# Output product of layer 0 from seven products of half blocks, in 19 of its 32 steps

## The chip, the cores and the metric

The kernel runs on one core of a Trainium2 chip. A core has TensorE (matmuls, PE in the profile), VectorE (DVE), ScalarE (ACT), GpSimd (POOL) and SyncE (SP, which issues DMAs). The metric is the device time of one execution in microseconds (us). Before the change the median of three runs is 2060.91 us (2059.85 to 2061.62).

## What is computed

Two transformer-like layers over 4 sequences of 512 tokens with 512 features, all in f32. Layer 0 adds to its input an attention and a mixture of experts. The attention has 16 heads of 128: every head sees a local window (the token's own block of 128 and the one before) and the eight best of 128 compressed entries; the two contexts are averaged. All heads together go through the output matrix Wo:

```python
merged = (ctx_sparse + ctx_local) * 0.5
out = merged.transpose(0, 2, 1, 3).reshape(Bq, Sq, NH * D) @ Wo + bo
...
x = x + _L0_attn_ref(xn, ...) + _L0_ffn_ref(xn, L0_ffn_Wr, L0_ffn_We, L0_ffn_be)
```

The product with Wo (2048 rows, 512 columns) is what the change touches. Layer 1, another attention and a second mixture of experts, stays as it is.

## The kernel before, in words

**Steps.** Layer 0's attention runs as 32 steps (list `steps`). A step i is a pair (g, b): g is one of 8 pairs of heads, b one of 4 sequences, and b runs fastest, so four steps share the weights of a head pair. In step i the kernel makes the scores and contexts of step i, the projections (queries, keys, values) of step i + 1, and pieces of the mixture of experts. From step 5 to step 22 each step handles two slots of 128 sorted token rows: `turn` (L517 to L519) transposes the gathered rows, `apply` (L529, L532) multiplies them with the expert's weights. GpSimd gathers rows and weights with indirect DMAs (L481) ahead of use. From step 23 on the experts' results are added up instead (L545, L852).

**A step in order.** `scores` (L749) makes for a head the compressed scores sp (L758) and the local scores st in two halves (L767). From sp, VectorE makes s (L761), finds the eight best (MAX, L779, and MATCH_REPLACE, L780) and masks the rest (L782 and L783, two operations on SBUF), and ScalarE takes the exponential (L784). From st, ScalarE makes lT (L771), and GpSimd multiplies it with a mask (L775). `context` (L798) multiplies with the values (L809 to L814), normalizes on ScalarE and VectorE (L818 to L827). `turn_context` (L831) transposes the context of a head on TensorE (trc, L834), and ScalarE copies it to cT[:, h, :] (L835). cT has 128 partitions (the head's features), 2 heads, 512 tokens.

**The output product.** `output` (L837) runs four times a step, once for each block of 128 tokens: two matmuls of 128 x 512, one for each head, accumulate in a PSUM bank op (L842), and VectorE adds op to acc (L845). acc is the residual stream, kept in SBUF for all 16 blocks of 128 tokens. Wo's part of the head pair is loaded once in four steps by `load_out` (L107, L109) into a single buffer; SyncE's queue holds that DMA until the step before has read the old one.

**Projections.** They are made from seven products of half blocks already (`project`, L650), each with two matmuls of 384 columns (L675). `first` makes the first four PSUM results of a step; VectorE's L710 and L711 take them out. `second`, `third`, `fourth` and `fifth` follow; the last takes its results out at L739 and rotates the keys (L585 to L588) after ScalarE has summed their squares (L575); GpSimd turns the sums into roots (L577, L578). In steps 5 to 23 the transposes of queries and keys (trq L695, trk L701) stand ahead of `fifth`. The sums of weight blocks that the seven products need are made by VectorE in `combine_weights` (L119), in steps with b = 2.

**PSUM.** `psum(tag, name)` hands out banks of 512 f32 for each partition: three buffers for "mm" (projections, expert products, output products), three for "sc" (scores, contexts), two for "tr" (transposes). A matmul into a fourth "mm" tile waits until VectorE has read one of the three.

**What sets the order.** The program text gives a priority; a scheduler at build time puts each engine's instructions in order, and each engine then runs its own queue strictly in that order, waiting on semaphores. The order is thus known before a run. TensorE's matmuls in f32 appear as two records each in the profile, each with a weight load (PEld).

Of the kernel before, what the change touches and what calls it, by code (L numbers as in the profile page):

```python
# [12 lines left out]
F32 = mybir.dt.float32  # L13
I32 = mybir.dt.int32
AF = mybir.ActivationFunctionType
ALU = mybir.AluOpType
# [4 lines left out]
P = 128  # L21
B, S, HID = 4, 512, 512
T = B * S
NT = T // P
TC = S // P
# [24 lines left out]
def two_layers(ctx: ExitStack, tc: tile.TileContext, a: dict, out: bass.AP, large: bass.AP):  # L50
# [3 lines left out]
    nc = tc.nc  # L54
    V, G, A, PE = nc.vector, nc.gpsimd, nc.scalar, nc.tensor
# [8 lines left out]
    wpool = layer0.enter_context(tc.tile_pool(name="wattn", bufs=2))  # L64
    const0 = layer0.enter_context(tc.tile_pool(name="const0", bufs=1))
    qp = layer0.enter_context(tc.tile_pool(name="qkv", bufs=2))
# [6 lines left out]
    def psum(tag, name):  # L73
        return ps.tile([P, 512], F32, tag=tag, name=name, bufs={"mm": 3, "sc": 3, "tr": 2}[tag])

    def load(pool, name, shape, src):
        t = pool.tile(shape, F32, tag=name, name=name, bufs=1)
        nc.sync.dma_start(out=t, in_=src)
        return t
# [8 lines left out]
    def load_block(g, nm, between=None):  # L88


        w = wpool.tile([P, KC, 3 * D], F32, tag=nm, name=f"{nm}_{g}", bufs=1 if nm == "wA" else 2)
        for f in range(2):
            nc.sync.dma_start(out=w[:, ts(f, 2), :],
                              in_=a[nm][g, ts(f, 2 * P), :].rearrange("(k p) c -> p k c", p=P))
            if between:
                between(nm, f)
        return w

    def load_later(g):

        w = load_block(g, "wB")
        b2 = wpool.tile([P, 2, 3 * D], F32, tag="b2", name=f"b2_{g}")
        for i, nm in enumerate(("bA", "bB")):
            nc.sync.dma_start(out=b2[:, i, :], in_=a[nm][g].partition_broadcast(P))
        return [[None, w], b2]

    def load_out(g):  # L107
        wo = wpool.tile([P, HG, HID], F32, tag="Wo", name=f"Wo_{g}", bufs=1)
        nc.sync.dma_start(out=wo, in_=a["Wo"][ds(g * HG * D, HG * D), :].rearrange("(h p) c -> p h c", p=P))  # L109
        return wo  # L110
# [11 lines left out]
            tc.keep_in_program_order(d)  # L122
        sums_w[g] = t2_, t3_, t4_

    sums_w, out_w = {}, {}
    wk = wv = bkv = cmask = lmask = eidx = row = part = None


    acc = keep.tile([P, NT, HID], F32, tag="acc", name="acc")
# [8 lines left out]
    def load_x(n):  # L138
        nc.sync.dma_start(out=acc[:, n, :], in_=x_v[:, n, :])
# [61 lines left out]
    def tables():  # L201

        for hs, w in ((0, 0), (1, 0), (2, 1)):
            tc.keep_in_program_order(G.tensor_tensor(t1[:, :, hs, :], cos[:, 0:TC], own_(w, TC, 0, R), ALU.mult))
            for half, other in ((0, 1), (1, 0)):
                tc.keep_in_program_order(G.tensor_tensor(t2[:, :, hs, ts(half, 32)], sin[:, 0:TC, ts(half, 32)], own_(w, TC, 32 * other, 32), ALU.mult))
# [252 lines left out]
    class Experts:  # L459
# [53 lines left out]
        def turn(self, i):  # L513
            x = self.x[i]
            tr = self.bank("tr", f"trm_{self.r.name}_{i}")
            for k in range(KC):
                PE.transpose(tr[:, ts(k, P)], x[:, ts(k, P)], ident)  # L517
            xT = self.pool.tile([P, KC, P], F32, tag="xT", name=f"xT_{self.r.name}_{i}")
            A.copy(xT, tr.rearrange("p (k t) -> p k t", k=KC))  # L519
            self.x[i] = xT  # L520
# [117 lines left out]
    steps = [(g, b) for g in range(NH // HG) for b in range(B)]  # L638
# [4 lines left out]
    def load_sums(i):  # L643

        for n in range(4):
            xs[n] = wk0.tile([P, 2, 256], F32, tag=f"x{n}", name=f"x{n}_{i}", bufs=1)
            if i >= B:
                nc.sync.dma_start(out=xs[n].rearrange("p k t -> p (k t)"), in_=xsd[steps[i][1], n])
# [182 lines left out]
    def turn_context(i, h, ctx_, cT):  # L831
        tr = psum("tr", f"trc_{i}_{h}")
        for t in range(TC):
            PE.transpose(tr[:, ts(t, P)], ctx_[:, t, :], ident)  # L834
        A.copy(cT[:, h, :], tr)  # L835

    def output(i, t, cT):  # L837
        g, b = steps[i]
        wo = out_w[g]
        op = psum("mm", f"op_{g}_{b}_{t}")  # L840
        for h in range(HG):
            PE.matmul(op, lhsT=cT[:, h, ts(t, P)], rhs=wo[:, h, :],  # L842
                      start=(h == 0), stop=(h == HG - 1))
        n = b * TC + t
        V.tensor_tensor(acc[:, n, :], acc[:, n, :], op, ALU.add)  # L845

    def combine(ex, n):
        rs = ex.gather(n)

        def add():  # L850
            for k in range(2):
                tc.keep_in_program_order(V.scalar_tensor_tensor(  # L852
                    acc[:, n, :], rs[k], ex.r.gate[:, k, n : n + 1], acc[:, n, :], ALU.mult, ALU.add
                ))
        return add
# [29 lines left out]
    def start_sequence(n):  # L885
        for f in layernorm(n, sp0, psum, n >= TC):
            f()
# [4 lines left out]
    for b in range(1, B):  # L892
        i = b - 2
# [77 lines left out]
    for n in range(3 * TC):  # L971
        i, t = 29 + n // TC, n % TC
        last = t + 2 if t < 3 else 5
        if i + 1 == len(steps) and t == 3:
            last = 4
# [14 lines left out]
    def rest():  # L990
        nonlocal wk, wv, bkv, cmask, lmask, eidx, row, part
        start_sequence(2)
        start_sequence(3)
        tables()
        for n in range(TC, TC + 2):
            load_x(n)
        wk = load(sp0, "wk", [P, KC, D], a["Wk"].rearrange("(k p) d -> p k d", p=P))
        wv = load(sp0, "wv", [P, KC, D], a["Wv"].rearrange("(k p) d -> p k d", p=P))
        bkv = sp0.tile([P, 2, D], F32, tag="bkv", name="bkv", bufs=1)
        nc.sync.dma_start(out=bkv[:, 0, :], in_=a["bk"].partition_broadcast(P))  # L1000
        nc.sync.dma_start(out=bkv[:, 1, :], in_=a["bv"].partition_broadcast(P))
        for n in range(TC + 2, 2 * TC):
            load_x(n)
        out_w[0] = load_out(0)
        cmask = load(const0, "cmask", [P, SEEN[TC - 1].stop], a["c_cmask_seen"])
        lmask = load(const0, "lmask", [P, 2, 2, P], a["c_lmask01"])
        for n in range(2 * TC, NT):
            load_x(n)
        eidx = load(const, "eidx", [P, E], a["c_eidx"])
        row = load(const, "row", [P, P], a["c_row"])  # L1010
        part = load(const, "part", [P, 1], a["c_part"])
# [25 lines left out]
    for i, (g, b) in enumerate(steps):  # L1037
        if b == 0:
            if g:
                out_w[g] = load_out(g)  # L1040
            if g + 1 < NH // HG:
                groups[g + 1] = load_later(g + 1)
        more = i + 1 < len(steps)
        turn_last = turn_keys
        now = qkT
        cT = qp.tile([P, HG, S], F32, tag="cT", name=f"cT_{g}_{b}", bufs=1)
        nc.sync.dma_start(out=cv0s[i % 2][96:P, 0:D], in_=cv[0:32, b, 0:D])
        em0, lT0 = scores(i, 0, now)
        turn_last(1)
        if more:  # L1050
            load_sums(i + 1)
            qkT, sums_x, first, second, third, fourth, fifth, turn_queries, turn_keys = project(i + 1)
            first()
            sums_x()
            if b == 2 and g + 1 in groups:
                groups[g + 1][0][0] = load_block(g + 1, "wA")
        run0((i, 0))
        em1, lT1 = scores(i, 1, now)
        sT0 = turn(i, 0, em0)
        run0((i, 1))  # L1060
        if more:
            second(0)
            turn_queries(0)
        ctx0 = context(i, 0, lT0, sT0, lv)
        if more:
            second(1)
        sT1 = turn(i, 1, em1)
        if more:
            third()
        if b == 2 and g + 1 in groups:  # L1070
            combine_weights(g + 1)
        run0((i, 2))
        ctx1 = context(i, 1, lT1, sT1, lv)
        turn_context(i, 0, ctx0, cT)
        run0((i, 3))
        if more:
            fourth()


            if 5 <= i < 24:  # L1080
                turn_queries(1)
                turn_keys(0)
                fifth()
            else:
                fifth()
        turn_context(i, 1, ctx1, cT)
        if more and not 5 <= i < 24:
            turn_queries(1)
            turn_keys(0)
        run0((i, 3.5))  # L1090
        for t in range(TC):
            output(i, t, cT)
        run0((i, 4))
    scratch.close()
    layer0.close()
# [208 lines left out]
    left = {n: 2 for n in range(NT)}  # L1304
# [159 lines left out]
    for g in range(NG):  # L1464
        b, j = groups1[g]
# [32 lines left out]
    last = [psum1("st", f"o1_{n0 + t}", 2) for t in (0, 2)]  # L1498
    last = [last[t // 2][:, t % 2, :] for t in range(TC)]
# [709 lines left out]
```

## Time and profile before

| what | before |
|---|---|
| median of the runs | 2060.91 us |
| the profiled execution | 2062.1 us |
| its span, first to last instruction | 2060.0 us |
| mean granted TensorE clock | 0.996 |
| ScalarE busy | 867.8 us (42%) |
| GpSimd busy | 750.8 us (36%) |
| output product: matmul records, weight loads | 512, 512 |
| adds of the output product | 128, 87.4 us |
| DMA moved | 267.23 MB, mean 130 GB/s |

The profile gives for each engine the time in which an instruction of it ran. A group line has the line number, the engine, the operation, out<-in by names, the shape and the count; then the busy time, the mean of one in ns, and the idle time of the engine just before those instructions, with what ended it. In the order of time a line has its start in us from the start of the span, its length, and in brackets the idle time before it and what released it. Durations of neighbours on one engine overlap a little, so that rates are read from start to start. One of the 19 steps lasts 45.8 us; the stretch shown in the prediction is that around the output product of one of them.

### The profile page before, as it was taken

The page shows a single profiled execution, that of the slowest core. Times are in us where ns is not written, and L with a number is a line of the kernel's source. Part 1 is how long each engine was busy: PE and PEld are TensorE (multiplying, and loading weights), DVE is VectorE, ACT ScalarE, POOL GpSimd, SP SyncE. Part 2 cuts the span into 40 slices and gives each one's busy share as a digit, 9 for nine tenths or more (in the row PEclk, how much of TensorE's full clock was granted, in tenths as well). Part 3 has the DMA queues.
Part 4 walks back from the last instruction along what each step waited for, and adds up shares of the span by engine and source line. Part 5 has one row for each costly group of instructions (what it writes and reads, how often), then busy time and mean ns, then how long its engine had stood idle before and what let it go on. Part 6 is the DMA issues. An engine that isn't in the chain of part 4 may idle for free.

```text
span 2060.0 us, 27976 instructions
## 1 busy us (share of the span) xinstructions
PE 2000.5 (97%) x9130; PEld 1199.1 (58%) x9130; DVE 1450.3 (70%) x3543; ACT 867.8 (42%) x2600; POOL 750.8 (36%) x761
## 2 busy tenths in 40 slices
PE   7999999999999999999999999999999999999997
PEld 4666666666666666666666666666334445445442
DVE  7889967666766666676667787787595555557775
ACT  4554444344444443444444454454243432433332
POOL 4422244443323333334334444353114432432550
PEclk9999999999999999999999999999999999999999
DMA  7101133333332343244453222121317775773551
GB/s 251 68 34 60 42 125 133 125 108 113 125 132 101 110 154 103 93 136 162 179 182 113 72 82 75 51 73 62 120 36 260 255 253 200 261 251 119 154 165 51
DMA packets 98906, 267.23 MB, mean 130 GB/s; under 512 B 14400, under 2 KB 27840, under 8 KB 87488
## 3 DMA queue, kind: packets, MB, share of 16 engines
q0 software_dynamic: 27072, 148.91, 21.3%
q1 hardware_dynamic: 70528, 114.34, 16.5%
q10 hardware_dynamic: 1152, 2.10, 0.3%
q8 instruction: 75, 1.23, 0.2%
q14 instruction: 79, 0.65, 0.1%
HBM read 222.05 MB, written 42.73 MB: 129 GB/s over the span
## 4 chain that ended last, share of the span: by engine, by line
PE 80%; DVE 8%; POOL 3%; ACT 3%; issue 2%; DMA 2%; DVEq 0%; ACTq 0%; POOLq 0%
PE p L675 25%; PE hp_r L529 12%; PE op L842 11%; PE st L767 4%; PE sp L758 3%; PE st L1249 2%; PE cx L1263 2%; PE qp L1225 2%; PE ca L811 2%; DVE pS L1269 2%; PE o L1332 1%; PE trq L695 1%; PE trm_r L517 1%; PE trk L701 1%; PE cc L814 1%
## 5 line engine op out<-in xcount | busy, mean ns | idle before, releaser
L842 PE MATMUL op<-Wo,cT 128*128 128x512 f32 x512 | 229.0, 596 | 1.5 <-ACT cT L835 1.1
L529 PE MATMUL hp_r<-we_r,xT_r 128*128 128x512 f32 (+1 forms) x592 | 225.6, 596 | 3.1 <-ACT xT_r L519 2.2
L481 POOL DMA_INDIRECT xr_r<-xnd,rows_r x72 | 88.7, 1232 | 333.5 <-PE trm_r L517 298.6
L775 POOL TENSOR_TENSOR lT<-lT,lmask 128x512 f32<-128x512 f32 (+1 forms) x128 | 155.8, 1229 | 145.9 <-ACT lT L771 145.6
L675 PE MATMUL p<-wT,x 128*128 128x384 f32 x512 | 179.5, 493 | 0.8 <-DVE wT L119 0.8
L675 PE MATMUL p<-wB,x 128*128 128x384 f32 x512 | 176.2, 488 | 2.7 <-DVE u L731 2.6
L675 PE MATMUL p<-wA,xnT 128*128 128x384 f32 x512 | 173.2, 490 | 0.2 <-DVE u L710 0.2
L575 ACT ACTIVATE sq<-qb 128x128 f32<-128x128 f32 x384 | 118.9, 310 | 90.1 <-DVE qb L724 45.2
L842 PEld LDWEIGHTS op<-Wo,cT 128*128 128x128 f32 x512 | 92.3, 190 | 109.3 <-issue 80.9
L1251 ACT ACTIVATE pT<-st 128x1024 f32<-128x1024 f32 x128 | 123.3, 1013 | 62.5 <-PE st L1249 56.8
L529 PEld LDWEIGHTS hp_r<-we_r,xT_r 128*128 128x128 f32 (+1 forms) x592 | 83.2, 170 | 100.0 <-issue 93.4
L845 DVE TENSOR_TENSOR acc<-acc,op 128x512 f32<-128x512 f32 x128 | 87.4, 684 | 70.0 <-PE op L842 69.6
L675 PEld LDWEIGHTS p<-wB,x 128*128 128x128 f32 x512 | 93.7, 190 | 66.8 <-issue 9.6
L675 PEld LDWEIGHTS p<-wT,x 128*128 128x128 f32 x512 | 94.5, 193 | 63.2 <-issue 6.3
L675 PEld LDWEIGHTS p<-wA,xnT 128*128 128x128 f32 x512 | 95.4, 192 | 60.5 <-issue 2.5
L689 ACT ACTIVATE qb<-qb,ss 128x128 f32<-128x128 f32 x256 | 81.9, 390 | 107.5 <-POOL ss L578 104.4
L519 ACT COPY xT_r<-trm_r 128x512 f32<-128x512 f32 x72 | 41.8, 580 | 193.1 <-PE hp_r L529 183.1
L771 ACT ACTIVATE lT<-st,ss 128x256 f32<-128x256 f32 (+1 forms) x128 | 46.8, 447 | 175.4 <-PE st L767 175.4
L767 PE MATMUL st<-qkT 128*128 128x256 f32 (+1 forms) x512 | 108.5, 354 | 1.5 <-ACT qkT L702 1.5
L545 POOL DMA_INDIRECT row_r<-yd,slot_r x64 | 74.4, 1163 | 94.2 <-DVE row_r L1366 36.6
L767 PEld LDWEIGHTS st<-qkT 128*128 128x128 f32 x512 | 92.1, 190 | 11.9 <-ACT qkT L702 1.7
L578 POOL TENSOR_TENSOR ss<-ss,nhalf 128x6 f32<-128x6 f32 x64 | 96.0, 1500 | 5.3
(360 smaller groups left out, 4313.0 us busy)
## 6 DMA issues: line engine op xcount, KB each, us to landing
x<-xsd SPq DMA_DIRECT2D x112, 256.0 KB
yd<-yr_r SPq DMA_DIRECT2D x72, 256.0 KB
wA<-in_wA SPq DMA_DIRECT2D x16, 384.0 KB
wB<-in_wB SPq DMA_DIRECT2D x16, 384.0 KB
xnd<-xn SPq DMA_DIRECT2D x24, 256.0 KB
accd<-acc SPq DMA_DIRECT2D x18, 256.0 KB
acc<-in_x SPq DMA_DIRECT2D x16, 256.0 KB
Wo<-in_Wo SPq DMA_DIRECT2D x8, 512.0 KB
```

The source lines that it names most:

```text
L481: G.indirect_dma_start(out=out, out_offset=None, in_=src, in_offset=at_rows(idx))
L529: PE.matmul(hp[ts(h, m), :], lhsT=xT[:, k, ts(h, m)], rhs=w[:, ts(k, HID)], start=(k == 0), stop=(k == KC - 1))
L545: G.indirect_dma_start(out=x, out_offset=None, in_=self.yd, in_offset=at_rows(self.r.slot[:, k, n : n + 1]))
L575: A.activation(sq, x[:, h, :], AF.Square, accum_out=ss[:, h : h + 1])
L578: pin(G.tensor_tensor(ss, ss, nhalf[:, 0:n], ALU.pow))
L675: PE.matmul(p, lhsT=x[:, k, ts(c, P)], rhs=w[:, k, :], start=(k == 0), stop=(k == 1))
L689: A.activation(x[:, j, :], x[:, j, :], AF.Copy, scale=sq[t][:, j : j + 1])
L767: PE.matmul(st[:, ds((t % 2) * 256, n)], lhsT=qkT[:, HG + h, ts(t, P)], rhs=qkT[:, h, ds(t * P, n)], start=True, stop=True)
L775: G.tensor_tensor(dst, dst, lmask.rearrange("p a w j -> p (a w j)")[:, 0:n], ALU.mult)
L842: PE.matmul(op, lhsT=cT[:, h, ts(t, P)], rhs=wo[:, h, :], start=(h == 0), stop=(h == HG - 1))
L845: V.tensor_tensor(acc[:, n, :], acc[:, n, :], op, ALU.add)
L1251: A.activation(pt[:, ts(pair, 2), :], st, AF.Exp, scale=SCALE1)
```

## The change

In the 19 steps from i = 5 to i = 23 the product of a step (512 tokens by 256 features times 256 by 512) is cut in halves along each of the three dimensions, and made from seven products of half blocks. A product is two matmuls of 128 x 256 into the halves of one PSUM bank (one for each block of 128 tokens), over the 128 features of one head. `combine_out` makes the sums of Wo's blocks on VectorE, four operations of 256 elements: three into a new tile WoT, and one in place over a block of Wo. It is called where i = 5 and where b = 0 in steps 6 to 23. `output7` returns two functions. `before` makes the one product that needs head 0 alone, ahead of `turn_context` for head 1. `rest` makes the other six, four sums of cT's blocks on VectorE (three into a new tile cS, one in place over a block of cT), and the adds. Partial results are accumulated on in the banks x and z after VectorE has added them to acc: x is added three times, the last time to both column halves of the second pair of token blocks at once (1024 elements, its operand broadcast), z twice, y and w once. A step has seven adds instead of four. Outside these steps `output` stays. To make room for the new tiles, the SBUF scratch for the descriptors of GpSimd's DMAs is set to 8192 bytes a partition.

```diff
--- before.py
+++ after.py
@@ -122,7 +122,7 @@
             tc.keep_in_program_order(d)
         sums_w[g] = t2_, t3_, t4_
 
-    sums_w, out_w = {}, {}
+    sums_w, out_w, out_t = {}, {}, {}
     wk = wv = bkv = cmask = lmask = eidx = row = part = None
 
 
@@ -843,6 +843,70 @@
                       start=(h == 0), stop=(h == HG - 1))
         n = b * TC + t
         V.tensor_tensor(acc[:, n, :], acc[:, n, :], op, ALU.add)
+
+    low, high = slice(0, 256), slice(256, HID)
+
+    def combine_out(g):
+
+        wo = out_w[g]
+        b11, b12, b21, b22 = (wo[:, h, c] for h in range(2) for c in (low, high))
+        t = wpool.tile([P, 3, 256], F32, tag="WoT", name=f"WoT_{g}", bufs=1)
+        V.tensor_tensor(t[:, 0, :], b12, b11, ALU.subtract)
+        V.tensor_tensor(b12, b22, b12, ALU.subtract)
+        V.tensor_tensor(t[:, 1, :], b22, t[:, 0, :], ALU.subtract)
+        V.tensor_tensor(t[:, 2, :], t[:, 1, :], b21, ALU.subtract)
+        out_t[g] = t
+
+    def output7(i, cT):
+
+        g, b = steps[i]
+        wo, wt = out_w[g], out_t[g]
+        a11, a21, a12, a22 = (cT[:, h, c] for h in range(2) for c in (low, high))
+        banks = {}
+
+        def product(x, left, right, last=True):
+            new = x not in banks
+            if new:
+                banks[x] = psum("mm", f"o{x}_{g}_{b}")
+            p = banks[x]
+            for c in range(2):
+                PE.matmul(p[:, ts(c, 256)], lhsT=left[:, ts(c, P)], rhs=right, start=new and c == 0, stop=True,
+                          skip_group_check=True)
+
+        def add(x, half, cols, op=ALU.add):
+            p = banks[x].rearrange("p (c f) -> p c f", c=2)
+            own = acc[:, ds(b * TC + 2 * half, 2), :]
+            if cols is None:
+                own = own.rearrange("p c (f x) -> p c f x", f=2)
+                p = p.unsqueeze(2).to_broadcast([P, 2, 2, 256])
+            else:
+                own = own[:, :, cols]
+            V.tensor_tensor(own, own, p, op)
+
+        def before():
+            product("x", a11, wo[:, 0, low], False)
+            add("x", 0, low)
+
+        def rest():
+            s = qp.tile([P, 3, 256], F32, tag="cS", name=f"cS_{g}_{b}", bufs=1)
+            s1, s2, s4 = (s[:, n, :] for n in range(3))
+            product("y", a12, wo[:, 1, low])
+            V.tensor_tensor(s1, a21, a22, ALU.add)
+            V.tensor_tensor(s2, s1, a11, ALU.subtract)
+            product("w", a22, wt[:, 2, :])
+            add("y", 0, low)
+            V.tensor_tensor(a21, a11, a21, ALU.subtract)
+            product("x", s2, wt[:, 1, :], False)
+            V.tensor_tensor(s4, a12, s2, ALU.subtract)
+            add("x", 0, high)
+            product("z", s1, wt[:, 0, :], False)
+            add("w", 1, low, ALU.subtract)
+            product("x", a21, wo[:, 0, high])
+            add("z", 1, high)
+            product("z", s4, wo[:, 1, high])
+            add("x", 1, None)
+            add("z", 0, high)
+        return before, rest
 
     def combine(ex, n):
         rs = ex.gather(n)
@@ -1072,6 +1136,8 @@
         run0((i, 2))
         ctx1 = context(i, 1, lT1, sT1, lv)
         turn_context(i, 0, ctx0, cT)
+        if i == 5 or b == 0 and 5 < i < 24:
+            combine_out(g)
         run0((i, 3))
         if more:
             fourth()
@@ -1083,13 +1149,20 @@
                 fifth()
             else:
                 fifth()
+        seven = 5 <= i < 24
+        if seven:
+            before, rest_ = output7(i, cT)
+            before()
         turn_context(i, 1, ctx1, cT)
         if more and not 5 <= i < 24:
             turn_queries(1)
             turn_keys(0)
         run0((i, 3.5))
-        for t in range(TC):
-            output(i, t, cT)
+        if seven:
+            rest_()
+        else:
+            for t in range(TC):
+                output(i, t, cT)
         run0((i, 4))
     scratch.close()
     layer0.close()
@@ -2192,7 +2265,7 @@
     }
     arrays.update(_constants())
 
-    nc = _bacc.Bacc("TRN2", target_bir_lowering=False, num_devices=1)
+    nc = _bacc.Bacc("TRN2", target_bir_lowering=False, num_devices=1, dynamic_dma_scratch_size=8192)
     feeds, aps = {}, {}
     for name, v in arrays.items():
         v = np.ascontiguousarray(v)
```

In the order that the scheduler makes of this, TensorE runs the matmuls of x (first time), the transposes of head 1, sp and the first matmul of st of the next step, then y, w, x, z, the second matmul of st, x, z, and the other two of st. VectorE's L761 and the first MAX and MATCH_REPLACE of the next step stand between the adds. ScalarE copies cT for head 1 after three of the four squares of L575, where it was after one. The sums of `combine_out` stand behind the first L710 of a step with b = 0, but for the first time, where three of them stand in step 4 and the fourth behind step 4's output products.

## Prediction

> **What bounds the kernel now.** I read the page first: busy shares, the slices of the span, the costliest groups.
>
> ```profile
> PE 2000.5 (97%) x9130; PEld 1199.1 (58%) x9130; DVE 1450.3 (70%) x3543; ACT 867.8 (42%) x2600; POOL 750.8 (36%) x761
> PE   7999999999999999999999999999999999999997
> L842 PE MATMUL op<-Wo,cT 128*128 128x512 f32 x512 | 229.0, 596 | 1.5 <-ACT cT L835 1.1
> L845 DVE TENSOR_TENSOR acc<-acc,op 128x512 f32<-128x512 f32 x128 | 87.4, 684 | 70.0 <-PE op L842 69.6
> ```
>
> TensorE (PE) is busy 97% of the span, the output product had 1.5 us of idle before it in 512 records, and the add after it (L845) waited 69.6 us for PE, not the reverse. Then the busy times by stretch, for the 19 steps that the change touches (their adds run from 314 to 1141 us).
>
> ```profile
> core 0: us, PE busy (x) PEld busy (x) DVE busy (x) ACT busy (x) POOL busy (x), PEclk, DMA share, GB/s
> 440.00:1100.00 660.00, 660.00 (x2946) 424.09 (x2944) 438.75 (x1154) 286.03 (x1000) 232.15 (x221) 1.00 0.38 132
> ```
>
> PE has no gap in 660 us, at full clock; DVE is at 66%. So a matmul column taken out shortens a step at once, until another engine makes PE wait. Whether one does is read in the order of time of one step (period 45.8 us); first PE from the last projection product of a step to the next step's first four.
>
> ```profile
> 720.88 2.75 PE L675 MATMUL p<-wB,x 128*128 128x384 f32 x8
> 723.47 0.60 PE L834 MATMUL trc<-ident,ctx 128*128 128x128 f32 x4
> 723.90 7.11 PE L842 MATMUL op<-Wo,cT 128*128 128x512 f32 x16
> 730.85 1.05 PE L758 MATMUL sp<-ckT,qkT 128*128 128x32 f32 x8
> 731.74 1.68 PE L767 MATMUL st<-qkT 128*128 128x256 f32 x8
> 733.26 0.60 PE L701 MATMUL trk<-ident,lv 128*128 128x128 f32 x4
> 733.70 5.33 PE L675 MATMUL p<-wA,xnT 128*128 128x384 f32 x16
> 738.86 0.60 PE L517 MATMUL trm_r<-ident,xr_r 128*128 128x128 f32 x4
> ```
>
> Starts give the rates, since durations overlap: the 16 records of op take 723.90 to 730.85, 0.434 each (each f32 matmul is two records). st, six of 256 and two of 128 columns, takes 1.52; a 128-column record is 0.11 (trk, 0.44 for four), so 256 columns take (1.52 - 0.22) / 6 = 0.217, exactly half of 512. DVE in the same time, and the GpSimd (POOL) multiplication beside it:
>
> ```profile
> 726.23 0.68 DVE L845 TENSOR_TENSOR acc<-acc,op 128x512 f32<-128x512 f32 x1
> 727.62 0.69 DVE L845 TENSOR_TENSOR acc<-acc,op 128x512 f32<-128x512 f32 x1 [0.71 <-PE op L842]
> 729.34 0.69 DVE L845 TENSOR_TENSOR acc<-acc,op 128x512 f32<-128x512 f32 x1 [1.03 <-PE op L842]
> 731.05 0.69 DVE L845 TENSOR_TENSOR acc<-acc,op 128x512 f32<-128x512 f32 x1 [1.03 <-PE op L842]
> ...
> 734.16 1.18 DVE L782 TENSOR_TENSOR rep<-s,rep 128x320 f32<-128x320 f32 x1
> 735.38 1.17 DVE L783 SCALAR_TENSOR_TENSOR s<-rep,s 128x320 f32<-128x320 f32 x1
> 736.47 0.55 DVE L710 TENSOR_TENSOR u<-p,b 128x384 f32<-128x384 f32 x1
> ```
>
> ```profile
> 733.73 2.47 POOL L775 TENSOR_TENSOR lT<-lT,lmask 128x512 f32<-128x512 f32 x2 [1.33 <-ACT lT L771]
> ```
>
> Between the adds DVE idles 0.7 to 1.0 us: room for the new work. The nearest danger is L710 at 736.47: it frees the PSUM buffer that PE's fourth projection product (from 737.57) takes, the pool "mm" having three.
>
> **What the Trainium skill says.** "TensorE: Matmul & The Clock Gate", Step-by-step: weight loads are pulled ahead of matmuls in flight. The trace agrees: a load beside 217 ns matmuls shows 190 ns and PE stays gapless. "VectorE: DVE Perf Modes", Why PSUM operands drop a tier: an f32 operation with a PSUM operand runs at one element per cycle; here 768 against 256 elements costs 0.54 us more, 1.05 ns per element. "SBUF — State Buffer", two separate sides: GpSimd and a DVE operation with two SBUF inputs exclude each other for a whole instruction. Agrees: L782 and L783 above last 1.18 and 1.17 beside L775, where each takes 0.48 at its least. "DMA: Bandwidth & Descriptors", SWDGE vs HWDGE vs iDMA: GpSimd's descriptor rings lie in a piece of SBUF, which the change halves; no view of the trace shows how full it is.
>
> **The change part by part.**
>
> *TensorE.* Out: 16 records of 512 columns, 6.95 us a step. In: 7 products x 2 row blocks x 2 records = 28 of 256 columns, 28 x 0.217 = 6.08. Gain 0.87 us a step if nothing waits, 16.5 over 19 steps. More weight loads (28 for 16) cost nothing: they hide under 0.217 as in st, and even under the 0.11 of the transposes.
>
> *DVE.* Prices by start-to-start times: 512 elements with PSUM 0.59 (L532 at 719.19, next at 719.78), 256 from SBUF 0.34 (r_k, 724.26 to 724.60), 768 0.88, so 1024 about 1.15. Out: 4 x 0.59 = 2.36. In: six adds of 512, 3.54; the broadcast add of 1024, 1.15; four sums of 256, 1.36; together 6.05, so 3.7 more a step, 70 us in all. The idle time from 723 to 739 is 0.35 + 0.80 + 0.71 + 1.03 + 1.03 + 0.20 + 0.73 = 4.85 us: it fits in sum. Does it fit in order? The instruction order of the changed program is known: PE gets x (a11), transposes, sp, the first st, then y, w, x (s2), z (s1), the second st, x (a21), z (s4), the rest of st. In the clock of the step above:
> - PE: x 723.47, transposes 724.34, sp 724.77, st 725.66, y 726.09, w 726.96, x (s2) 727.83, z (s1) 728.70, st 729.57, x (a21) 730.00.
> - ACT copies cT after three squares instead of one (the order says so): the second square needs lv at 724.23, so they end at 725.19, the copy at 725.77. y needs it by 725.9. Just in time.
> - DVE: first x add 725.0; s1 when cT is there, 725.85; L588 726.2; s2 726.54, ready 726.97 against 727.83; a21 726.88; y add 727.22; s4 727.81; w add 728.15; L761 728.74; second x add 729.18 to 729.87. The product x (a21) writes the bank which that add reads, so it starts at about 729.9 to 730.1 instead of 730.00, the weight load waiting too: I take a stall of 0.1 a step.
> - z add 729.87 to 730.46; then the first of MAX and MATCH_REPLACE, 0.76; the broadcast add 731.2 to 732.35 (its product ends 730.97, and DVE follows PE by 0.2, as at L845); last z add to 732.94; the rest of MATCH_REPLACE, 0.93; L782 from 733.87. By then POOL's first L775 is over, since st's first half is done at 730.0; the second (1.00 us) runs 733.4 to 734.4. So L782 ends at 734.75 and L783 at 735.2, less blocked than before, and L710 is done at 735.75. The fourth projection product wants its buffer at 732.92 + 3 x 1.29 = 736.79: cover of 1.0 us. If that cover is gone, every us of DVE lateness beyond it is PE's.
> - POOL's L577 and L578 (0.42 and 1.03 us) now stand beside s2 and a21, which have two SBUF inputs. Bounds: 0, or all 1.45 us. Nearest row: with L578 beside four L119 sums in the b = 2 step, L578 stretched to 1.93 and the L119 kept 0.95. I take 0.
>
> Net gain 0.87 - 0.10 = 0.77 a step.
>
> *combine_out.* Four DVE sums per head pair, five times, 1.4 us each. In the order they stand after the next step's first L710 (the first time in step 4), so the fourth product's buffer is not behind them; what is behind them, the second L710 and the rotation, feeds the trq transposes over 3 us later (qb scaled at 744.6, used at 748.05). They wait for the DMA of Wo: it is issued at 593.72, and DMA is busy until 597.1; the sums want it at about 599. Issued 1 us later, it still arrives first. SyncE's queue holds this DMA until Wo is last read, about 1 us later; the wB, x and cv loads behind it have many us. I take 0; 0 to 5 us in all.
>
> *Descriptor scratch halved.* Gathers are issued 13 to 16 us ahead of use (xr_r at 739.75, used 756.44). Taken as 0; a gain is excluded, since less room makes no gather earlier; a loss needs over 10 us of delay per gather.
>
> *Sum.* 19 x 0.77 = 14.6 us. The profiled execution took 2062.1 (span 2060.0), the median of the runs is 2060.9; the difference is 0.06%. 2060.9 - 14.6 = 2046.3.
>
> **The rivals.**
> - *DVE is late by more than I work out* (a slower handover, a dearer broadcast add), and the wait at x (a21) or at the fourth product grows by 0.4 us. For it: the first has no cover. Against: the second has 1.0. Gain 0.37 x 19 = 7: 2053.9.
> - *The change doesn't arrive at the end*: after 1141 us something fixed in time, such as a load, sets the end. For: PE waits in places there (142 of 150 us busy from 1300 to 1450). Against: those waits are for ACT and DVE, which shift with PE. 2060.9.
> - *Slower: POOL holds DVE.* L577 and L578 hold the shared access while s2 waits, 1.45 us. Then s2 is ready at 728.4, and the second x add ends at 731.3 instead of 729.87, so x (a21) starts 1.4 later in all: 0.87 - 1.45 = -0.58, times 19, +11: 2072. It decides from a delay of 0.8 us. For: L782 shows such blocking. Against: the L119 rows.
>
> **How the numbers follow.** Forecast (2043.4 to 2050) 0.66; DVE late 0.17; no arrival 0.09; slower 0.08. Low end: all 16.5 and 1 us of the ACT wait in the last of the 19 steps. High end 2055: it takes in most of the late case and leaves out the last two, 0.17 and a little below. A measurement of this kernel tells 0.2% (4 us) from no change: faster 0.83, within 0.09, slower 0.08.
>
> **What would show it.** Right: PE gapless in 440 to 1100, step period 45.0 instead of 45.8; PE busy about 1984; DVE about 1525; few waits of PE at the new products, 0.1 us each, behind the second x add. Wrong: idle before L675 released by DVE u (the buffer), s2 starting after 727.5 in the step's clock, L577 and L578 unstretched beside stretched sums, or a broadcast add well over 1.2 us.

## The result, and the profile after

The changed kernel takes 2042.11 us (median of four runs, 2039.16 to 2044.51), the kernel before beside it 2060.38 (2059.76 to 2061.62): a ratio of 0.991, 95% interval 0.9893 to 0.9927. That is 18.3 us faster. I had predicted 14.6 us and 2046.3, with a low end of 2043.4; the median lies 1.3 us below that end. Two more sets of runs of the same kernel gave 2043.96 and 2042.08.

The lines of the page that answer to those of before:

```profile
PE 1983.6 (97%) x9358; PEld 1243.6 (61%) x9358; DVE 1506.5 (74%) x3696; ACT 868.5 (43%) x2600; POOL 746.3 (37%) x761
L842 PE MATMUL op<-Wo,cT 128*128 128x512 f32 x208 | 93.7, 595 | 0.4 <-DVE lv L739 0.4
```

The add of the new products is L884; its costliest group, from the list of all groups, is that of product x:

```profile
L884 DVE TENSOR_TENSOR acc<-acc,ox 128x512 f32<-128x512 f32 (+1 forms) x57 | 48.9, 857 | 0.0
```

PE is busy 16.9 us less (2000.5 to 1983.6) and its share is still 97%. 304 of the 512 records of op are gone. The adds hardly wait for PE any more: the groups of L884 have 1.1 us of idle before them together (all of it before the adds of y), where L845 had 70.0. The stretch in the middle, as before:

```profile
440.00:1100.00 660.00, 660.00 (x3207) 470.48 (x3206) 493.92 (x1315) 292.86 (x1023) 235.81 (x227) 1.00 0.39 134
```

PE has no gap here either, and DVE went from 438.75 to 493.92 us of 660. One step in order of time, on PE:

```profile
714.72 1.03 PE L873 MATMUL ox<-Wo,cT 128*128 128x256 f32 x4
...
719.07 1.03 PE L873 MATMUL ox<-WoT,cS 128*128 128x256 f32 x4
719.94 1.03 PE L873 MATMUL oz<-WoT,cS 128*128 128x256 f32 x4
720.80 0.59 PE L767 MATMUL st<-qkT 128*128 128x256 f32 x2
721.23 1.03 PE L873 MATMUL ox<-Wo,cT 128*128 128x256 f32 x4
722.10 1.03 PE L873 MATMUL oz<-Wo,cS 128*128 128x256 f32 x4
...
724.05 5.33 PE L675 MATMUL p<-wA,xnT 128*128 128x384 f32 x16
```

Products are named by bank and left operand: x (a21) is the third product into bank x, that of the block a21 of cT. Every product takes 0.86 from start to start (714.72 to the transposes at 715.58, 719.07 to 719.94), so a record of 256 columns is 0.216. Product x (a21) at 721.23 starts exactly when st before it is through (720.80 + 0.43), and z follows after 0.87: there is no stall where I had put one. DVE in the same step:

```profile
720.35 0.68 DVE L884 TENSOR_TENSOR acc<-acc,ox 128x512 f32<-128x512 f32 x1
...
722.36 1.21 DVE L884 TENSOR_TENSOR acc<-acc,ox 128x1024 f32<-128x1024 f32 x1
...
725.02 1.06 DVE L782 TENSOR_TENSOR rep<-s,rep 128x320 f32<-128x320 f32 x1
726.11 0.49 DVE L783 SCALAR_TENSOR_TENSOR s<-rep,s 128x320 f32<-128x320 f32 x1
726.52 0.55 DVE L710 TENSOR_TENSOR u<-p,b 128x384 f32<-128x384 f32 x1
```

The second x add, the one that x (a21) waits for, ends at 721.03, which is 6.31 us after the step's first product; I had worked out 6.40.

**Where the time came from.** The first transposes of the contexts (trc) of a step make a marker that every kernel here has. From that of step 5 to that of step 24, these are the 19 changed steps and nothing else:

| kernel | trc of step 5 | trc of step 24 | the 19 steps | against before |
|---|---|---|---|---|
| before | 301.57 | 1164.41 | 862.84 | |
| changed | 300.56 | 1146.16 | 845.60 | -17.24 |
| changed, second set of runs | 301.56 | 1147.16 | 845.60 | -17.24 |
| changed, third set of runs | 300.71 | 1146.54 | 845.83 | -17.01 |

So 17.2 us of the gain lie in these steps, 0.91 a step (one period is now 44.87 us, 659.94 to 704.81, before 45.78). Step 4, ahead of the first marker, is 0.29 us longer than before (44.11 for 43.82), for which see `combine_out` below. The two profiled executions differ by 22.9 us of span (2060.0 and 2037.1), which is more than the change made: from the last trc of layer 0 to the end, work that the change doesn't touch, one took 622.5 us and the other 619.1, and over the executions shown here it is 619.1 to 623.5. The difference of the medians, 18.3 us (interval 15.0 to 22.0), agrees with 17.2.

### The profile page after: what moved, and what is told of

The parts are those of the page before. It is cut to its first block, busy times and chain, and to the rows that moved or that the text cites. A ratio compares the mean times of both kernels' runs of the same rounds, so it can differ in the third digit from the quotient of the medians.

```text
span 2037.1 us, 28573 instructions
## 1 busy us (share of the span) xinstructions
PE 1983.6 (97%) x9358; PEld 1243.6 (61%) x9358; DVE 1506.5 (74%) x3696; ACT 868.5 (43%) x2600; POOL 746.3 (37%) x761
## 4 chain that ended last, share of the span: by engine, by line
PE 81%; DVE 9%; ACT 3%; POOL 2%; issue 2%; DMA 1%; ACTq 0%; DVEq 0%; SPq 0%; POOLq 0%
PE p L675 25%; PE hp_r L529 12%; PE op L842 4%; PE st L767 4%; PE sp L758 2%; PE st L1322 2%; PE ox L873 2%; PE qp L1298 2%; PE cx L1336 2%; PE ca L811 2%; DVE pS L1342 2%; PE o L1405 2%; PE oz L873 2%; PE trm_r L517 1%; PE trq L695 1%
## 5 line engine op out<-in xcount | busy, mean ns | idle before, releaser
L775 POOL TENSOR_TENSOR lT<-lT,lmask 128x512 f32<-128x512 f32 (+1 forms) x128 | 152.6, 1200 | 129.1 <-ACT lT L771 128.9
L575 ACT ACTIVATE sq<-qb 128x128 f32<-128x128 f32 x384 | 118.9, 310 | 96.2 <-DVE qb L724 45.8
L767 PE MATMUL st<-qkT 128*128 128x256 f32 (+1 forms) x512 | 114.7, 354 | 1.5 <-ACT qkT L702 1.5
L578 POOL TENSOR_TENSOR ss<-ss,nhalf 128x6 f32<-128x6 f32 x64 | 95.4, 1490 | 5.3
L842 PE MATMUL op<-Wo,cT 128*128 128x512 f32 x208 | 93.7, 595 | 0.4 <-DVE lv L739 0.4
L577 POOL TENSOR_SCALAR ss<-ss 128x6 f32<-128x6 f32 x64 | 31.0, 485 | 164.3 <-ACT sq L575 163.9
L675 PE MATMUL p<-wT,xnT 128*128 128x384 f32 x256 | 88.0, 486 | 0.0
```

The source lines that it names most:

```text
L575: A.activation(sq, x[:, h, :], AF.Square, accum_out=ss[:, h : h + 1])
L578: pin(G.tensor_tensor(ss, ss, nhalf[:, 0:n], ALU.pow))
L675: PE.matmul(p, lhsT=x[:, k, ts(c, P)], rhs=w[:, k, :], start=(k == 0), stop=(k == 1))
L767: PE.matmul(st[:, ds((t % 2) * 256, n)], lhsT=qkT[:, HG + h, ts(t, P)], rhs=qkT[:, h, ds(t * P, n)], start=True, stop=True)
L775: G.tensor_tensor(dst, dst, lmask.rearrange("p a w j -> p (a w j)")[:, 0:n], ALU.mult)
L842: PE.matmul(op, lhsT=cT[:, h, ts(t, P)], rhs=wo[:, h, :], start=(h == 0), stop=(h == HG - 1))
```

## Experiments

My theory after the result (call it columns): the gain is TensorE's columns alone, 28 records of 0.216 for 16 of 0.434 on average, or 0.90 a step, and nothing waits at the new products. Rivals: a part of it is outside the 19 steps, from the smaller scratch; the stall of 0.1 is there and something else gives more; DVE's new work costs time by itself.

### The same kernel again, and the scratch alone

> The changed kernel again, for a second profile and more times. Theory T (the gain is the TensorE time taken out, 0.90 us a step with no stall, 17.2 us over 19 steps, and about 1 us of a wait in step 31 that goes): the stretch from the first to the last of the 19 steps is 17.2 us shorter than before again, and the median is 17 to 19.5 us below that of before. Rival R (what was gained beyond 14.6 us is spread of the runs, above all of layer 1): the median is within 1.5 us of 14.6 below.

It took 2043.96 us (ratio 0.9913, 0.99 to 0.9927), 17.1 us less than before on the same chip. The third set, later and beside other runs:

> The changed kernel once more, to set the size of its gain beside the others on one chip: by the step anchors of the traces (17.2 us in the 19 steps) 2043 to 2045; if the first four runs were the rule, 2041 to 2043.

It took 2042.08 us (ratio 0.9909, 0.9894 to 0.9924). The kernel before with nothing but the scratch halved:

```diff
-    nc = _bacc.Bacc("TRN2", target_bir_lowering=False, num_devices=1)
+    nc = _bacc.Bacc("TRN2", target_bir_lowering=False, num_devices=1, dynamic_dma_scratch_size=8192)
```

> The kernel before with the descriptor scratch at 8192 bytes alone. Theory T: no difference, within 1.5 us of before (about 2060.4). Rival S (the freed SBUF, other addresses or the shorter ring are worth the part of the gain that the matmuls don't explain): 1 to 4 us faster, or slower if gathers wait for the ring.

It took 2059.5 us (ratio 0.9993, 0.9984 to 1.0001), and its 19 steps 862.85 us against 862.84. The scratch costs nothing and brings nothing in these steps.

### Fewer of the steps

```diff
-        if i == 5 or b == 0 and 5 < i < 24:
+        if i == 5 or b == 0 and 5 < i < 14:
-        seven = 5 <= i < 24
+        seven = 5 <= i < 14
```

> The seven products in the first nine of the 19 steps alone (i from 5 to 13), scratch halved as in the changed kernel. Theory columns (0.90 us a step, and at most 1 us that has nothing to do with the number of steps): 8.1 to 9.1 us faster than before, 2052 to 2053. Rival (0.77 a step, the rest of the gain a fixed amount of 2.5 to 3.5 us outside these steps): 9.4 to 10.4 us faster, 2050.5 to 2051.5. Rival of the arrival (something late in the program takes back a fixed part): under 7 us faster, over 2054.

What it changes in the computation: in steps 14 and 15 the whole product uses a Wo in which one block has already been replaced by a difference. The instructions are those of a whole product, so the time can be read as meant. It took 2050.35 us (ratio 0.9949, 0.9936 to 0.9961), 10.8 less than before, which is the figure of the rival with a fixed part. The trace says otherwise: its 19 steps last 855.11 us, 7.73 less than before, 0.51 in step 5 and 0.905 in each of the other eight. The 3.1 us between the two figures lie outside all changed steps, and the interval of the ratio (8.0 to 13.2 us) reaches down to the theory's 8.1. The times alone did not decide here; the markers did.

### TensorE's columns put back

Product y is made twice, so that TensorE has 32 records of 256 (6.91 us) where it had 16 of 512 (6.95), and all of DVE's new work stays:

```diff
-            for c in range(2):
+            for c in (0, 1, 0, 1) if x == "y" else (0, 1):
```

> The changed kernel with product y made twice, the second over the first, so that TensorE has 32 records of 256 columns a step, 6.91 us as against 6.95 before, and all of VectorE's new work stays. Theory T: nearly all of the gain is gone, 1 us below before at most plus the 1 us of step 31 (2058.5 to 2060). Rival O (the new order, the accumulation in PSUM, or less blocking of VectorE's L782 and L783 by GpSimd bring part of the gain): still 3 us or more below before.

It took 2064.46 us (ratio 1.0015, 1.0008 to 1.0021). The gain was gone, as columns says, but the kernel was 3.4 us slower than before, and its 19 steps 4.28 us longer. The order of TensorE shows why. The scheduler had put x (a21) straight behind z, and the st that stood between them in the changed kernel behind it:

```profile
731.40 1.03 PE L873 MATMUL oz<-WoT,cS 128*128 128x256 f32 x4
732.43 1.13 PE L873 MATMUL ox<-Wo,cT 128*128 128x256 f32 x4
733.40 0.59 PE L767 MATMUL st<-qkT 128*128 128x256 f32 x2
```

x (a21) starts 1.03 after z where 0.86 would do, and takes 0.97 itself: 0.28 a step. A first attempt to hold that order (its edit is left out here) held the wrong instructions, and x (a21) stayed directly behind z:

> Product y made twice again (four matmuls instead of two, so that TensorE has 32 records of 256 columns in these steps, 6.91 us at 0.216, against 6.95 before), but with TensorE's order held as in the changed kernel: the second st half stays between product z (s1) and product x (a21). All of VectorE's new work stays. Theory columns (the gain is TensorE's records alone, and the first such run lost another 0.2 us a step only because the scheduler put x (a21) directly behind z (s1)): no stall at x (a21), some 16.4 us slower than the changed kernel (19 x 0.864), within 1.5 us of the kernel before: 2059.5 to 2061. Rival (VectorE's 70 us more cost about 0.2 us a step wherever they stand): as in the first run, 2063.5 to 2065.

It took 2064.15 us (ratio 1.0016, 1.001 to 1.0023), its 19 steps 866.90 us, 4.06 more than before, with the same two gaps. This says nothing between the theories, since the order was not the one meant. The second attempt makes x (a21) wait in the order for the st matmul (of its edit, the lines that add this dependence):

```diff
+                if t == 1 and h == 0 and i - 1 in third_x:
+                    tc.add_manual_dep(third_x[i - 1].ins, d.ins.name, mybir.DependencyInfo(
+                        mybir.DependencyClass.NoSync, mybir.DependencyReason.DATA), reason="order")
```

> Product y made twice, as in the two runs before, but now product x (a21) waits in TensorE's order for the second matmul of the scores st, so that this stands between z (s1) and x (a21) as it does in the changed kernel (in the run that meant to hold the order it stood behind x (a21) all the same). Theory columns and cover: no stall at x (a21), TensorE has 32 records of 256 for 16 of 512, so the 19 steps last as long as before, 0 to 0.8 us less, and the whole run is within 2 us of the kernel before, 2059.5 to 2061.5; step period 45.73 to 45.78. Rival (VectorE's 70 us more cost TensorE about 0.25 us a step whatever stands there): 4 us over the kernel before, 2064 to 2065.5, period 46.0.

It took 2061.03 us (ratio 1.0, 0.9992 to 1.0009). With st back in its place, the gaps are gone:

```profile
728.12 1.03 PE L876 MATMUL oz<-WoT,cS 128*128 128x256 f32 x4
728.98 0.59 PE L767 MATMUL st<-qkT 128*128 128x256 f32 x2
729.41 1.03 PE L876 MATMUL ox<-Wo,cT 128*128 128x256 f32 x4
730.28 1.03 PE L876 MATMUL oz<-Wo,cS 128*128 128x256 f32 x4
```

Its step period is 45.73 us (44.87 + 0.86), its 19 steps last 861.61, 1.2 us less than before. So DVE's new operations cost nothing in such a step, and putting TensorE's columns back takes the gain away but for 1.2 us: columns is confirmed for the greater part, and what a wait at x (a21) costs depends on one matmul of 0.43 us standing there.

The 1.2 us that stay show that "alone" was too much. In the kernel before, 0.434 is an average: the records of op start 0.43 apart, but for the third, which takes 0.51 (724.76 to 725.27). It is the first that reads head 1, and its weight load waits for ScalarE's copy of cT:

```profile
724.10 0.58 ACT L835 COPY cT<-trc 128x512 f32<-128x512 f32 x1 [0.28 <-PE trc L834]
```

```profile
724.74 0.30 PEld L842 LDWEIGHTS op<-Wo,cT 128*128 128x128 f32 x2 [0.64 <-ACT cT L835]
```

This holds for each of the steps 5 to 22 (in step 23 the wait is longer). In the changed kernel x (a11), which reads head 0 alone, and the next step's sp and st stand in the time of that copy, and in these steps no record of the new products is longer than the others. Sixteen records of op without the wait take 6.87 us, the 28 new ones 6.04: of the 0.91 us a step 0.82 are columns, or 15.6 us in the 19 steps, and 0.08 are this wait, about 1.5 us. The kernel with y made twice agrees: 32 records take 6.91, 0.04 more than the 6.87, the wait of 0.08 is gone, and the period is 0.04 shorter than before.

### The add made later

How much room has x (a21)? Operations on DVE that change nothing (the maximum of a block of acc with itself) are put ahead of the second x add, with TensorE's order held (by lines left out here) to that of the changed kernel: in the traces it is the same from the first matmul to the last. One of 512 elements:

```diff
+            own = acc[:, ds(b * TC, 2), high]
+            for _ in range(1):
+                tc.keep_in_program_order(V.tensor_tensor(own, own, own, ALU.max))
```

> One more VectorE operation of 512 elements from SBUF (the maximum of acc's own block with itself, 0.59 us from start to start) ahead of the second x add, TensorE's order held; L761 (0.40) falls behind that add, so the add comes 0.2 us later than in the changed kernel. Theory cover (the changed kernel has some 0.15 us in hand at product x (a21)): a stall of 0.05 us a step at most 0.1: 0.5 to 2 us slower than the changed kernel, 2044 to 2046. Rival (the stall of 0.1 that I predicted is there, hidden in the records): the whole 0.2 us a step shows, 3.8 us slower, 2047 to 2048.

It took 2046.49 us (ratio 0.9924, 0.9911 to 0.9936); its 19 steps last 848.36 us, 2.76 more than the changed kernel's, or 0.145 a step on average and 0.16 in an ordinary step (45.03 for 44.87). This lies between what the two theories said (0.05 to 0.1, and 0.2), so the room is smaller than the 0.15 us that I had read off. The trace shows the size of it:

```profile
722.72 0.59 PE L767 MATMUL st<-qkT 128*128 128x256 f32 x2
723.21 1.13 PE L876 MATMUL ox<-Wo,cT 128*128 128x256 f32 x4
724.18 1.03 PE L876 MATMUL oz<-Wo,cS 128*128 128x256 f32 x4
```

x starts 0.06 late (723.21 instead of 722.72 + 0.43), but takes 0.97 instead of 0.86. The weight loads (PEld) tell why; first the changed kernel, then this one:

```profile
721.08 0.78 PEld L873 LDWEIGHTS ox<-Wo,cT 128*128 128x128 f32 x4
```

```profile
723.21 0.73 PEld L876 LDWEIGHTS ox<-Wo,cT 128*128 128x128 f32 x4 [0.29 <-DVE acc L887]
```

It is the weight load that waits for the add: it starts 0.05 us after the add's end (721.03) in the changed kernel, still 0.15 ahead of its matmul, and 0.06 after it (722.47 + 0.68 = 723.15) in this one, at the same time as its matmul, which is then 0.1 us longer. Two operations of 256 elements, with which L761 stands ahead of the add as in the changed kernel, so that the add shifts further:

```diff
+            own = acc[:, ds(b * TC, 1), high]
+            for _ in range(2):
+                tc.keep_in_program_order(V.tensor_tensor(own, own, own, ALU.max))
```

> The changed kernel with two more VectorE operations of 256 elements a step (an in-place maximum of acc with itself) ahead of the second x add, L761 too before it, and TensorE's order held to that of the changed kernel: the second x add ends 0.7 to 0.8 us later. It measures the cover at the product x (a21), for which the prediction allowed none and a stall of 0.1 us. The add ended 0.20 us ahead of that product in the changed kernel. Theory T (cover of about 0.1 to 0.2 us, no more): a stall of 0.5 to 0.65 us a step, 9.5 to 12.5 us slower than the changed kernel, about 2052 to 2055. Rival C (the wait is looser than the trace shows, other work covers it): less than 4 us slower.

It took 2055.2 us (ratio 0.9973, 0.9962 to 0.9983); its 19 steps last 857.45 us, 11.85 more than the changed kernel's. The wait is now named:

```profile
726.74 0.59 PE L767 MATMUL st<-qkT 128*128 128x256 f32 x2
727.69 1.13 PE L876 MATMUL ox<-Wo,cT 128*128 128x256 f32 x4 [0.36 <-DVE acc L887]
```

The kernels fit one sum: the loss a step is the end of the add (in the kernel before, of ScalarE's copy), plus 0.16 us (0.05 to the start of the weight load, 0.11 for the load that is no longer hidden), less the time at which the waiting product could have started otherwise, if that is positive. What was lost is read from the periods, or from start to start where the order is another.

| kernel | end + 0.16 | could start | by the sum | measured |
|---|---|---|---|---|
| changed | 721.19 | 721.23 | 0 | 0 |
| one operation of 512 | 723.31 | 723.15 | 0.16 | 0.16 |
| two of 256 | 727.80 | 727.17 | 0.63 | 0.63 |
| y twice, no st between | 732.55 | 732.26 | 0.29 | 0.28 |
| before, third record of op | 724.84 | 724.76 | 0.08 | 0.08 |

The 0.16 can be read from the two kernels with late adds alone, so their rows describe more than they test; the last two rows are the test. By this sum the changed kernel has 0.04 us to spare at x (a21).

### All 32 steps

```diff
-        if i == 5 or b == 0 and 5 < i < 24:
+        if i == 0 or b == 0 and 0 < i < 32:
-        seven = 5 <= i < 24
+        seven = 0 <= i < 32
```

> The seven products in all 32 steps. Theory columns: 13 more steps of at most 0.90, 11.7 us, less what VectorE (busier there: the combination of the experts' results from step 23 on) makes TensorE wait; TensorE has some idle in steps 24 to 31 already. I expect about half: 2036 to 2040. Rival (VectorE is the bound in steps 0 to 4 and 24 to 31, so the additions cost what the columns bring): 2043 to 2048.

It took 2062.3 us (ratio 1.0008, 1.0 to 1.0016): all that the 19 steps bring is lost in the other 13, which neither of my numbers foresaw. The 19 steps are as in the changed kernel (845.65 us). From the trc of step 0 to that of step 5 it takes 229.5 us, the changed kernel 219.8, and the steps from 24 on are about 12.6 us longer. Busy times of those two stretches (PE first, DVE third):

```profile
82.00:312.00 230.00, 216.57 (x1116) 157.58 (x1115) 200.29 (x606) 107.25 (x374) 70.58 (x77) 0.99 0.19 64
...
1157.00:1442.00 285.00, 267.58 (x1369) 201.07 (x1367) 239.88 (x673) 131.18 (x464) 117.44 (x113) 0.99 0.21 66
```

PE idles 13.4 and 17.4 us in them, in the changed kernel 6.0 and 6.7 in the stretches that answer to them, and DVE is busy 87 and 84% of the time, in the steps with the gain 75% (637.6 of 845). In step 0 nothing of the next step's scores stands among the first five new products, and z (s1) waits 0.56 us for an add; in step 24 PE waits 1.12 us at trk for ScalarE's copy of cT. How much of the 22 us such waits make, and how much DVE's work, was not tried.

## Why the prediction was right or wrong

The main mechanism and the place were right; the gain was put 2.6 us too low (14.6, measured 17.2 in the 19 steps).

- **TensorE's columns: the sum right, a little small, and part of it by luck.** I took 0.217 for a record of 256 columns, and the trace has 0.2155 to 0.216 (0.86 to 0.87 for four); 16 records of 512 were 6.95. So 0.87 became 0.91, 0.7 us over 19 steps. But 6.95 held a wait of 0.08 for ScalarE's copy, which I had taken for the price of columns: a record of 512 costs 0.429, not 0.434, and columns alone bring 0.82. The new order removes the wait, so the error did not show in the sum. The extra weight loads cost nothing, as said: PE busy was to be about 1984, and is 1983.6.
- **The stall of 0.1 us at product x (a21): wrong, and the step that failed.** "I take a stall of 0.1 a step" came out as none. It made 1.9 of the 2.6 us. The measured handover would have given 0.03 with my own times (the add's end at 729.87, plus 0.16, against 730.00), and the add came 0.09 earlier than worked out. I had put a guess where the difference of two estimates was within their error, and kept only one side of it. The place was well chosen, though: with 0.04 us to spare it is the next thing to bind, as the two late adds show.
- **The order on DVE: right.** Counted from the step's first product, the broadcast add was to start at 7.73 and starts at 7.64 (and lasts 1.12 from start to start, for 1.15, a price that I had worked out from operations on SBUF alone); L782 at 10.40 and 10.30; L710 was to be done at 12.28 and is at 12.35. DVE's sum was too large, 70 us more where 56.2 were measured: in 440 to 1085 the mean of L783 fell from 830 to 516 ns and that of L782 from 1344 to 1223 in 28 instructions each, 12 us, where they now stand less beside GpSimd's L775 (in the step shown, L783 lasts 0.49 instead of 1.17). I had said "less blocked" and not counted it.
- **The cover of the fourth projection product: right but for one step.** The product could start at 724.05 + 3 x 1.29 = 727.92, and L710 ends at 727.07: 0.85 us, for 1.0. In step 5 it failed:

```profile
320.77 1.47 DVE L782 TENSOR_TENSOR rep<-s,rep 128x320 f32<-128x320 f32 x1
322.28 1.17 DVE L783 SCALAR_TENSOR_TENSOR s<-rep,s 128x320 f32<-128x320 f32 x1
323.37 0.55 DVE L710 TENSOR_TENSOR u<-p,b 128x384 f32<-128x384 f32 x1
```

Beside them GpSimd runs L954, two additions over acc of 2.5 us together, and then L775. L710 ends at 323.92, and plus 0.16 that is 0.41 later than 319.80 + 3 x 1.29 = 323.67. The sixteen records there take 5.57 from start to start instead of 5.17: 0.40 lost, by the same sum as at x (a21). It is why step 5 gains 0.50 only.
- **The scratch, GpSimd's L577 and L578 at nothing: right.** In the step shown L577 came at 722.19, 4 us behind the sums that it was to disturb, but in 15 of the 19 steps the two stand where I had put them: in one, L578 runs from 493.46 to 494.55, s2 from 493.24 and a21 from 493.57. Over all 19 steps the four sums last 417 to 427 ns, so none was held: the exclusion that the prediction reckoned with does not show at these small operations.
- **combine_out at nothing: right but for its first call.** The steps with combine_out (8, for one: 435.58 to 480.45) last 44.87 like the others. The first call has sums in step 4, one of them between VectorE's operations of L818; counted from the step's first trc, the last of these comes 0.21 us later than before and L731, for which PE waits, 0.28:

```profile
256.53 0.42 DVE L857 TENSOR_TENSOR WoT<-WoT,Wo 128x256 f32<-128x256 f32 x1
```

```profile
261.62 1.56 PE L675 MATMUL p<-wB,x 128*128 128x384 f32 x4 [0.36 <-DVE u L731]
```

  Up to this product both kernels keep step to 0.01 us, and from it on the changed one is 0.28 later. Every kernel here whose first call is that of step 5 has a step 4 of 44.10 or 44.11, and the one with the scratch alone 43.83.
- **The sum in hindsight:** 14.6, plus 1.9 for the stall that isn't there, plus 0.7 for the new products, less 0.4 in step 5: 16.8, against 17.2. The last two steps, 22 and 23, gained 1.14 and 1.12 (40.90 us for 42.05, 39.05 for 40.17) and make up the rest; in the third set step 22 gained 0.90. Step 4 takes 0.3 back outside the markers.
- **The rivals.** DVE late by 0.4 at x (a21) did not come by itself, but was made: with 0.6 us lost a step the kernel takes 2055.2. No arrival is out, since the 17.2 us reach the end. GpSimd holding DVE at s2 did not happen; it did at L782 in step 5.
- **The range** ended at 2043.4, the full gain of the columns and 1 us, with nothing for the spread of the medians. Three sets of runs of the changed kernel gave 2042.1, 2044.0 and 2042.1, so an end for what is at most 17.5 us of gain needed some 2 us more.

What stays open: the medians of these kernels show on average 0.9 us more gain than their 19 steps (from 0.8 less, with y made twice and st in place, to 3.1 more, with nine steps), and 0.3 more again where step 4 is counted. It lies in parts whose instructions are unchanged; layer 1 varies by 4.4 us between single executions, so these runs can't place it.

## What to carry to other kernels

Where one engine has no gap, a change that takes columns from it brings what the columns cost there, read from records that wait for nothing (0.429 here, where the average over a stretch with a wait gave 0.434), provided that every product which waits for another engine has something else standing between it and the work that it waits for: here one matmul of 0.43 us was worth 0.28 us a step. Price such a wait as the other engine's end plus the handover, less the time of the last own work ahead of it, and when this comes out near zero, put both sides of it into the range. The order that a scheduler chooses is part of that price: an edit that only doubled a product moved the covering matmul away. And compare kernels by a marker at both ends of the changed steps: two spans differed by 22.9 us where the change made 17.2.

## What the runs showed of the hardware that was not expected

A TensorE wait costs more than its length. "TensorE: Matmul & The Clock Gate", Step-by-step, says that weight loads are pulled ahead of matmuls in flight, and the traces agree wherever nothing waits. Where a matmul waits for VectorE, its weight load waits too and starts 0.05 us after the end of VectorE's record, so that 0.11 us of load are no longer hidden (the product's start to the next is 0.97 instead of 0.86 in all four kernels that wait at x (a21)). The start of the matmul alone shows 0.06 us of loss in the kernel with one late operation, where the step lost 0.16. Behind ScalarE's copy, in the kernel before, it is the same: the load starts 0.05 us after the copy's end, the matmul starts on time, and 0.08 us are lost though PE shows no idle time.
